# Seven products of quarters for the wide layers of five blocks instead of three, and larger steps of side work

## The chip, the cores and the metric

The kernel runs on one core of a Trainium2 chip. The metric is the device time of one execution in microseconds. A profile of one execution goes with it; its span runs from the first to the last instruction.

## What is computed

The program is a "macaron" layer on x of 4 x 1024 x 256 floats: half a feed-forward step, a mixing step over time, and half a feed-forward step again, each with a layer norm in front and a residual behind.

```python
def ffn(x):                      # w1_w, w2_w, h1_w, h2_w, w3_w hold -1, 0, 1
    h = silu(tlin(x, w1)) * tlin(x, w2)      # 256 -> 1024
    h = gelu(tlin(h, h1))                    # 1024 -> 1024, "wide"
    h = gelu(tlin(h, h2))                    # 1024 -> 1024, "wide"
    return tlin(h, w3)                       # 1024 -> 256
def attn(x):                     # a convolution over time by FFT, then one more product
    K = s4d_kernel(...)
    y = irfft(rfft(x) * rfft(K))[:L]
    return gelu(y) @ W.T + b
x = x + 0.5 * ffn(norm(x))
x = x + attn(norm(x))
x = x + 0.5 * ffn(norm(x))
```

Each `tlin` also scales its outputs by a vector.

## The kernel before, in words

**Blocks.** The 4096 tokens are cut into 8 blocks of 512 (TB). They pass the first feed-forward step as f0 to f7 and the second as g0 to g7; the mixing step of batch b, called m0 to m3, lies between: it needs f(2b) and f(2b+1), and g(2b), g(2b+1) need it. The last loop of `macaron_layers` runs `ffn` for f0 to g7 in turn. `x1` and `x2` in DRAM carry what one step hands to the next.

**A block.** Activations are split into a high and a low part, so that each product is done twice and summed in PSUM (`linear`, L366). The pair of first layers writes banks `pa` and `pb`; layers 2 and 3 (weights `h1_sb`, `h2_sb`) write `p2_...` and `p3_...`, eight pieces m of 128 output rows each, and each piece is 16 matmuls of 512 columns. A piece goes through Gelu on ACT (L418), a cast on ACT to the high part (L420) and a subtraction on DVE to the low part (`low_part`, L309). A following layer needs all eight. The last layer (L630) writes `po`. `ffn` calls `ahead()` and `tick()` after each piece of a wide layer. `ahead` takes a step of `prepare` for the next block: its load, its norm, its transposition through DRAM (`moved`, stored and loaded on POOL's queue).

**Blocks by sums.** In the last N_BY_SUMS blocks the wide layers are done by `winograd`: weights and activations are halved in both directions, and seven products of quarters (names `a`, `d`, `e` in `p2a_g`, `p3d_g` and so on, L484) replace eight. A product is 32 matmuls of 256 columns. Seven sums of weight quarters per wide layer are made once by `weight_sums` (16 steps in all; each second step stores seven pieces of `q` in DRAM, on POOL's queue). A block by sums loads 14 parts of 1 MB through SP's queue into four slots (`load_slot`, L581). Slots and activation tiles of these blocks take the place of `h1_sb` and `h2_sb`, so all sums must be made, and all mixing steps be done (an `assert` says so), when the first block by sums begins. Sums not made by then are made at that point, all at once.

**Side work.** `all_aside` is a generator that makes the convolution's spectrum (`kernel_steps`, `kernel_spectrum`) and then m0 to m3 in small steps. Work on DVE is counted in columns plus OP_WORK = 130 for each operation. Each `tick` allows STEP_WORK more of it (STEP_WORK_2 once f7 is done) and takes steps until that is used up, or until a step yields PAUSE, which means that it waits for something. At a PAUSE, also when side work has run out or waits for its block, one step of the "fillers" is taken if enough allowance is left. Fillers are the 16 steps of `weight_sums` and then 46 of `weight_checks`: 44 pieces of the weights are loaded once more from their inputs (`given`, SP's queue, 256 KB each), and DVE compares each with what the kernel uses (L156); for the pieces of h1 and h2 it is compared with its own sign, which ACT makes (L714). A value `bad` counts misses, and a plain version of the whole kernel runs behind an `If` where there are any.

**Order.** Within an engine the instructions stand in an order that the tile framework's scheduler fixes when the program is built; each engine works through its own in order. So where a matmul of the next layer needs a low part that comes late, the program may have put other matmuls in front of it.

**Lines that matter here:** L38 (steps), L44 (N_BY_SUMS), L309 and L366 (low part, products), L418 and L420 (Gelu, cast), L484 (products of quarters), L581 (weight parts), L630 (last layer), L703 and L714 (checks: load, sign), and `tick`.

Of the kernel before, what the change touches and what calls it, by code (L numbers as in the profile page):

```python
# [24 lines left out]
TB = 512  # L25
# [9 lines left out]

STEP_WORK, STEP_WORK_2, OP_WORK, MIN_WORK = 2500, 3000, 130, 300  # L38
PAUSE = "pause"
N_CHECKS = 44  # L40

N_BY_SUMS = 3  # L44
QT = TB // 2
QK = KH // 2
QW = HID // 2
# [62 lines left out]
def macaron_layers(  # L110
# [37 lines left out]
    work_done = 0  # L148
# [213 lines left out]
    def linear(ps, w, m, acts):  # L362
        n = len(acts)
        for k in range(n):
            for part in range(parts):
# [6 lines left out]
                )  # L372

    def ffn(xt, src, dst, blk, name, tick, ahead, final, by_sums):


# [21 lines left out]
        for layer, w in ((2, h1_sb), (3, h2_sb)):  # L398
            if by_sums:
                at = 0  # L400

                def step():
                    nonlocal at
                    at += 1
                    if at * KH // 14 > (at - 1) * KH // 14:
                        ahead()
                        if layer == 2 or at < 14:
                            tick()

                raw = winograd(raw, layer, name, step)  # L410
                continue
            hb = []
            for m in range(KH):
                ps = bank(f"p{layer}_{name}_{m}")
                linear(ps, w, m, ha)
                t = ring(f"h{layer}_{name}_{m}", parts, TB, dtype=wide)
                g = half(f"g{layer}_{name}_{m}") if split else t[:, 0, :]
                nc.scalar.activation(g, ps, AF.Gelu, scale=sc_sb[:, layer, m : m + 1])  # L418
                if split:
                    nc.scalar.copy(t[:, 0, :], g)  # L420
                    low_part(t, g)
                hb.append(t)
                ahead()
                if layer == 2 or m < KH - 1:
                    tick()
            ha = hb
# [91 lines left out]
    def winograd(raw, layer, name, step):  # L518
# [51 lines left out]
        (quarters[layer][i], f"w_{n}_{layer}_{i}")  # L570
        for n in range(N_BY_SUMS)
        for layer in range(2)
# [620 lines left out]
    done = []  # L1193
# [50 lines left out]
    fillers = chain(sums_of_weights, checks) if split else iter(())  # L1244
    late = late_pool = None
    ticks = 0
    allowed = 0

    def tick():


        nonlocal ticks, allowed, work_done
        ticks += 1
        allowed = min(allowed, work_done) + (
            STEP_WORK_2 if ("f", n_blocks - 1) in done else STEP_WORK
        )
        while work_done < allowed:
            at = work_done
            if next(aside, PAUSE) is PAUSE:
                if len(done) > 8 and allowed - work_done > OP_WORK + TB:  # L1260
                    next(fillers, None)
                break
            if work_done == at:
                work_done += MIN_WORK
# [8 lines left out]
    allowed = work_done  # L1273
    for n, (turn, blk) in enumerate(blocks):
# [8 lines left out]

        by_sums = split and n >= len(blocks) - N_BY_SUMS
        if by_sums and not slots:
# [93 lines left out]
```

## Time and profile before

| | |
|---|---|
| median of the runs | 1400.81 us (1399.09 to 1400.86, 3 runs) |
| the profiled execution | 1398.44 us, of which the span is 1396.7 |
| granted TensorE clock | 0.999 |
| matmuls of 512 columns in layers 2 and 3 | 1024 + 1024 in f0 to f7, 640 + 640 in g0 to g4 |
| Gelu behind them (L418), one | 689 ns on ACT |
| cast (L420) / low part (L309), one | 618 ns on ACT / 690 ns on DVE |
| a load of ACT's function table | 1283 ns |
| Sign of a check (L714) / compare (L156), one | 627 ns on ACT / 686 ns on DVE |
| weight part `w<-q`: count, size, issue to landing | 42, 1024 KB, 6.1 us |
| check load `given<-in_h_dram`: count, size, issue to landing | 32, 256 KB, 5.0 us |
| moved by DMA | 160.11 MB, mean 115 GB/s |

Times of single operations are means of groups of equal instructions. "Busy" of TensorE (PE) counts matmuls, which overlap, so that a matmul's own duration (391 ns for 512 columns) is longer than the step from one to the next; PEld are the loads of weights into the array, which run beside matmuls. An idle time of an engine is put down to the event that ended it.

The blocks begin at about these times of the span (first matmul of `pa`): f0 10, f1 90, f2 176, f3 259, f4 354, f5 441, f6 521, f7 622, g0 702, g1 796, g2 883, g3 977, g4 1063, g5 1157, g6 1238, g7 1314 us.

### The profile page before, as it was taken

To read this page: it belongs to the slowest core of one execution; us is meant where nothing else is said; L and a number is where in the kernel's file an instruction comes from. 1 tells how busy PE (TensorE), PEld (TensorE's weight loads), DVE (VectorE), ACT (ScalarE), POOL (GpSimd) and SP (SyncE) were. 2 spreads that over 40 slices of the span, in tenths; PEclk is the share of its full clock that TensorE was granted. 3 is DMA by queue.
4 is the path that set the end of the run, shared out by engine and by line. 5 is a ranking of instruction groups with operands and counts; after the bars stand their busy time and mean duration, and the time that the engine had idled before them with its cause. 6 is when DMAs were issued, how large, how long until landed. Compare 5 with 4: busy or idle time off the path is not lost.

```text
span 1396.7 us, 19695 instructions
## 1 busy us (share of the span) xinstructions
PE 1384.2 (99%) x7132; PEld 1182.6 (85%) x7132; DVE 932.8 (67%) x1766; ACT 766.8 (55%) x1227; POOL 297.0 (21%) x454
## 2 busy tenths in 40 slices
PE   9999999999999999999999999999999999999998
PEld 7888888888888888888888888888888888989998
DVE  6896667755637776377774569844597536877765
ACT  5986579644546445354353544534544445766664
POOL 4441022211312121521125301221112032121200
PEclk9999999999999999999999999999999999999999
DMA  9430101113131331532314414233132356959663
GB/s 355 127 131 21 41 16 46 31 30 96 50 108 36 106 90 54 203 92 83 76 46 162 134 37 128 61 91 106 53 95 50 100 143 237 332 169 320 193 221 114
DMA packets 121677, 160.11 MB, mean 115 GB/s; under 512 B 73873, under 2 KB 84113, under 8 KB 116193
## 3 DMA queue, kind: packets, MB, share of 16 engines
q1 hardware_dynamic: 99296, 99.41, 23.5%
q0 software_dynamic: 22000, 59.07, 13.7%
q8 instruction: 58, 0.95, 0.3%
q14 instruction: 51, 0.41, 0.1%
q10 hardware_dynamic: 272, 0.26, 0.1%
HBM read 120.95 MB, written 37.75 MB: 114 GB/s over the span
## 4 chain that ended last, share of the span: by engine, by line
PE 93%; DVE 3%; DMA 2%; ACT 1%; issue 0%; POOL 0%; SPq 0%; DVEq 0%; POOLq 0%; ACTq 0%
PE p_f L366 31%; PE p_g L366 19%; PE pa_f L366 4%; PE pa_g L366 4%; PE pb_f L366 4%; PE pb_g L366 4%; PE po_f L630 4%; PE po_g L630 4%; PE p2a_g L484 3%; PE p3a_g L484 3%; PE pi L1144 2%; PE pw L1169 2%; PE pf_m L966 2%; PE p2d_g L484 1%; PE p3d_g L484 1%; PE pk L893 1%
## 5 line engine op out<-in xcount | busy, mean ns | idle before, releaser
L366 PE MATMUL p_f<-h_f,h_sb 128*128 128x512 f32 x1024 | 237.1, 391 | 0.0
L366 PE MATMUL p_f<-ha_f,h_sb 128*128 128x512 f32 x1024 | 235.3, 390 | 0.0
L366 PEld LDWEIGHTS p_f<-h_f,h_sb 128*128 128x128 f32 x1024 | 191.8, 188 | 40.0 <-DVE h_f L309 0.3
L366 PEld LDWEIGHTS p_f<-ha_f,h_sb 128*128 128x128 f32 x1024 | 191.9, 188 | 39.8
L418 ACT ACTIVATE g_f<-p_f,sc_sb 128x512 f32<-128x512 f32 x128 | 87.7, 689 | 190.5 <-PE p_f L366 186.0
L309 DVE TENSOR_TENSOR h_f<-g_f,h_f 128x512 fp32r<-128x512 f32 x128 | 87.7, 689 | 143.3 <-ACT h_f L420 142.9
L418 ACT ACTIVATE g_g<-p_g,sc_sb 128x512 f32<-128x512 f32 x80 | 55.2, 690 | 174.6 <-PE p_g L366 165.0
L366 PE MATMUL p_g<-ha_g,h_sb 128*128 128x512 f32 x640 | 148.1, 391 | 0.0
L366 PE MATMUL p_g<-h_g,h_sb 128*128 128x512 f32 x640 | 147.9, 391 | 0.1
L366 PEld LDWEIGHTS p_g<-h_g,h_sb 128*128 128x128 f32 x640 | 120.0, 188 | 25.4 <-ACT h_g L420 0.5
L366 PEld LDWEIGHTS p_g<-ha_g,h_sb 128*128 128x128 f32 x640 | 120.0, 188 | 24.7
L309 DVE TENSOR_TENSOR h_g<-g_g,h_g 128x512 fp32r<-128x512 f32 x80 | 55.2, 690 | 111.8 <-ACT h_g L420 111.3
L339 POOL DMA_DIRECT2D moved<-sq_g x64 | 34.9, 552 | 314.9 <-DVE sq_g L156 313.8
L420 ACT CAST h_f<-g_f 128x512 fp32r<-128x512 f32 x128 | 78.3, 618 | 2.9
L418 ACT ACT_TABLE_LOAD x46 | 59.0, 1283 | 20.9 <-PE p_f L366 12.4
L366 PE MATMUL pa_f<-xt_f,w_sb 128*128 128x512 f32 x256 | 69.0, 390 | 0.7 <-DVE xt_f L321 0.7
L366 PE MATMUL pb_f<-xt_f,w_sb 128*128 128x512 f32 x256 | 68.8, 389 | 0.0
L366 PE MATMUL pa_g<-xt_g,w_sb 128*128 128x512 f32 x256 | 68.5, 389 | 0.0
L366 PE MATMUL pb_g<-xt_g,w_sb 128*128 128x512 f32 x256 | 68.4, 389 | 0.0
L392 DVE SCALAR_TENSOR_TENSOR g_g<-pb_g,sc_sb,g_g 128x512 f32<-128x512 f32 x64 | 47.7, 748 | 29.9 <-PE pb_g L366 19.2
L339 POOL DMA_DIRECT2D moved<-sq_f x56 | 30.8, 556 | 159.1 <-DVE sq_f L156 159.1
L392 DVE SCALAR_TENSOR_TENSOR g_f<-pb_f,sc_sb,g_f 128x512 f32<-128x512 f32 x64 | 47.3, 746 | 23.0 <-PE pb_f L366 15.9
(310 smaller groups left out, 2493.9 us busy)
## 6 DMA issues: line engine op xcount, KB each, us to landing
w<-q SPq DMA_DIRECT2D x42, 1024.0 KB, 6.1
q<-s POOLq DMA_DIRECT2D x40, 256.0 KB, 3.4
h_sb<-in_h_dram POOLq DMA_DIRECT2D x8, 1024.0 KB, 14.6
given<-in_h_dram SPq DMA_DIRECT2D x32, 256.0 KB, 5.0
kr<-k_hat SPq DMA_DIRECT2D x20, 256.0 KB, 2.7
ki<-k_hat SPq DMA_DIRECT2D x20, 256.0 KB, 2.9
xr_f<-in_x_dram SPq DMA_DIRECT2D x64, 64.0 KB, 2.5
q<-h_sb POOLq DMA_DIRECT2D x16, 256.0 KB, 5.8
```

Of the source, the lines that this page charges most:

```text
L309: return nc.vector.tensor_tensor(t[:, 1, :], src, t[:, 0, :].bitcast(F32), ALU.subtract)
L339: stores.dma_start(moved[k].rearrange("(c r) a q -> a r c q", r=SQ)[a], sq[a * SQ : (a + 1) * SQ].rearrange("r c j s -> r c (j s)"),)
L366: nc.tensor.matmul(ps, w[:, k, m * P : (m + 1) * P], acts[k][:, part, :], start=(k == 0 and part == 0), stop=(k == n - 1 and part == parts ...
L392: nc.vector.scalar_tensor_tensor(g if split else t[:, 0, :], pb, sc_sb[:, 1, m : m + 1], g, ALU.mult, ALU.mult)
L418: nc.scalar.activation(g, ps, AF.Gelu, scale=sc_sb[:, layer, m : m + 1])
L420: nc.scalar.copy(t[:, 0, :], g)
L484: nc.tensor.matmul(ps[:, e * QT : (e + 1) * QT], weights[:, c, m * P : (m + 1) * P], ops[c // 2][:, part, c % 2 * QT : (c % 2 + 1) * QT], ...
L630: nc.tensor.matmul(ps[:, n * n_t : (n + 1) * n_t], w3_sb[:, k, o * P : (o + 1) * P], act(k, part, n * n_t, (n + 1) * n_t), start=(k == ord ...
L893: nc.tensor.matmul(pk[0:NA, at + i, :, :].rearrange("p h b -> p (h b)"), a[:, i].rearrange("p a b -> p (a b)"), qd[d1 // per_tile][:, at + ...
L966: nc.tensor.matmul(ps[e][:, part, :], m[:, e, part, :], rows_of(q + JQ * e), start=True, stop=True)
L1144: nc.tensor.matmul(banks[dc][e][:, q * P : (q + 1) * P], vs[q + JQ * e][:, part, dc * P : (dc + 1) * P], m[:, e, part, :], start=(part == ...
L1169: nc.tensor.matmul(ps[:, e * D : (e + 1) * D], yts[dc][j // JQ][:, (j % JQ + e) * P : (j % JQ + e + 1) * P], wt_sb[:, dc, :], start=(dc == 0),
```

## The change

N_BY_SUMS goes from 3 to 5: g3 and g4 are done by sums too, so the mixing steps and the sums of weights have to be made two blocks earlier. The allowance of a tick grows from 2500 to 3200 columns, and from 3000 to 3400 once f7 is done. At a PAUSE up to two filler steps are taken instead of one, as long as the allowance lasts.

```diff
-STEP_WORK, STEP_WORK_2, OP_WORK, MIN_WORK = 2500, 3000, 130, 300
+STEP_WORK, STEP_WORK_2, OP_WORK, MIN_WORK = 3200, 3400, 130, 300
...
-N_BY_SUMS = 3
+N_BY_SUMS = 5
...
             if next(aside, PAUSE) is PAUSE:
-                if len(done) > 8 and allowed - work_done > OP_WORK + TB:
-                    next(fillers, None)
+                for _ in range(2):
+                    if len(done) > 8 and allowed - work_done > OP_WORK + TB:
+                        next(fillers, None)
                 break
```

What a filler step does is unchanged: the same 16 steps of sums and 46 of checks are made once.

## The prediction

> **What bounds the kernel now.** I read four views, in this order. First the page's totals and its 40 slices: which engine is full, and where.
>
> ```profile
> PE 1384.2 (99%) x7132; PEld 1182.6 (85%) x7132; DVE 932.8 (67%) x1766; ACT 766.8 (55%) x1227; POOL 297.0 (21%) x454
> ...
> PE   9999999999999999999999999999999999999998
> PEld 7888888888888888888888888888888888989998
> DVE  6896667755637776377774569844597536877765
> ACT  5986579644546445354353544534544445766664
> ...
> PEclk9999999999999999999999999999999999999999
> ```
>
> TensorE is full from end to end at full clock, so the time is the sum of its matmuls plus what it waits. The other rows are below 7 on average, but reach 8 and 9 in slices 2 to 4, 7 and 25: there they are almost the bound. Only in the last six slices does PEld reach 9: those are the blocks by sums.
>
> Second, the chain of waits, in order of time: what a pair of wide layers costs in both forms, and the last layer behind it.
>
> ```profile
> 455.57 58.03 PE p_f L366 x256
> 513.60 7.25 PE po_f L630 x32
> ...
> 1306.31 7.68 PE po_g L630 x64
> 1328.52 3.83 PE p2a_g L484 x32
> 1332.35 3.84 PE p2d_g L484 x32
> ```
>
> Third, the busy time by stretch for the blocks g5, g6, g7, the three already done by sums, each from its first matmul to the next block's.
>
> ```profile
> 1157.40:1237.50 80.10, 77.94 (x577) 73.87 (x576) 59.62 (x110) 56.16 (x107) 12.85 (x20) 1.00 0.81 283
> 1237.50:1313.80 76.30, 76.30 (x580) 73.62 (x580) 57.33 (x108) 50.77 (x96) 13.44 (x21) 1.00 0.73 241
> 1313.80:1390.00 76.20, 76.15 (x578) 73.43 (x576) 49.05 (x77) 48.23 (x91) 8.89 (x11) 1.00 0.45 157
> ```
>
> The columns are length, then busy time of PE, PEld, DVE, ACT, POOL, then clock, DMA share, GB/s. The same matmuls take 80.1 us in g5 and 76.2 in g6 and g7. Fourth, the waits of g5 alone (1157 to 1238) say why:
>
> ```profile
> DVE given L156 <- ACT sign L714: 7.0, 5, 2.1
> ...
> ACT sign L714 <- DMA given<-in_h_dram: 5.2, 5, 1.4
> ```
>
> Fifteen weight checks run in g5. Their 256 KB loads stand in SP's queue just behind 1 MB loads of weight parts and land after 6.8 us (median), against 3.3 in g3 and g4. ACT, which works in order, sits on a check's Sign while casts for the next product stand behind it. DVE waits next, and then TensorE, about 4 us in all. Over the blocks before g5, TensorE's only visible waits are 0.7 us at the first matmuls and 0.3 in f2.
>
> **The change, part by part.**
>
> *Two more blocks by sums (g3, g4).* Each drops 256 + 32 matmuls of 512 columns: 58.03 + 7.25 = 65.28 us by the chain, 227 ns each. Each gains 14 products of 32 matmuls of 256 columns at 3.84 us (120 ns each), and 64 in the last layer at 7.68: 53.76 + 7.68 = 61.44. That is 3.84 us a block, **7.7 us** for two, and all of it on the engine that sets the end. The Trainium skill, "TensorE: Matmul & The Clock Gate", in the part "Wait — 56ns, not 53.3ns?", prices a warm matmul at its columns by 2.4 GHz plus about 2.5 ns: 215.7 ns for 512 columns, 109.2 for 256. By that, 1024 x 109.2 - 576 x 215.7 = -12.4 us. The trace has 120, not 109, and PEld is busy 27.0 of 27.0 us in the products (1355 to 1382): weight loads, twice as many per column, fill the stage. I take the trace.
>
> The added DVE and ACT work lies beside these matmuls: g7 has the same work at 49 us DVE and 48 ACT of 76, g6 with seven checks 57 and 51, and neither waits. The 28 more loads of 1 MB on SP follow the pattern of g6 and g7 too, each hidden by four slots.
>
> *Larger steps (2500 to 3200, 3000 to 3400), two fillers at a pause.* These have to bring all side work in front of g3, since the weights h1, h2 are given up there. Going through the program block by block, the last mix ends in g2, all 16 steps of weight sums are done by f7, and of 62 filler steps 61 are done by g2 (25 of them in g2) and one in g3. So nothing is left to drain at the entrance to g3. Three costs follow.
>
> (a) *g5's wait goes.* No check's load stands among weight loads any more: 80.1 - 76.2 = **3.9 us** gained. Ends: 0 (if it belongs to the first block by sums rather than to the checks) and 4.1. The waits name the checks, so 3.9.
>
> (b) *g2 takes 25 filler steps, mostly pairs.* Per layer piece of 3.63 us a pair adds two Signs (0.63 each) to ACT's 0.69 + 0.62, so 2.6 us, and two compares (0.69) to DVE's 0.69, so 2.1: both fit. Each pair's 512 KB in 3.6 us is 144 GB/s, with no weight loads about. What can go wrong is the second load of a pair, needed right after the first: ACT and the casts and Gelus behind Sign would wait, then TensorE. Below: 0, as g4 with its ten steps shows (no Sign waits for a load there). Above: g5's rate, 3.9 x 25 / 15 = 6.5 us. Nearest is g4, since the 19-buffer ring lets loads run some ticks ahead; I take 0.3. SP's queue in g2 also holds the mix's x1 rows and the next blocks' x behind those loads; none is due before g5.
>
> (c) *f0 to g1 get denser.* A tick goes with 3.63 us of wide-layer matmuls (58.03 / 16). 3200 units are about five 512-column DVE operations: 5 x 0.61 (their spacing in the chain) = 3.05, plus low part 0.61 and about 0.5 for the next block: 4.2 us, where 2500 gave 3.5. So ticks in a row without a pause fall behind; pauses and side matmuls give it back. By counted instructions times row durations, DVE has 695 us up to g2's third layer against 930 of PE (before: 729 against 1090 up to g4): full only in places. In f0, between the last low part of the first layer and that of the third, DVE gets 12 more operations of 512 columns and four of 256: about 8 us on top of 49.2 busy in 58.2 (24.2 to 82.4). Part of the 9 us of idle there are waits for ACT that stay. Before, the last low part ended at 86.0, 3.8 us behind its matmuls; 2 to 5 more make 6 to 9. The program's PE order puts 26 matmuls (5.9 us) in between, where it was 16: a wait of 0 to 3, I take 1.8. In f1's third layer ACT gets 11 table loads at 1.30, 16 Gelus and casts at 0.69 and 0.62, nine Exp/Sin at 0.62, eight tap copies at 0.2: 32.0 us against 30.1 of PE; order there leaves 6.4 us: I take 0.7. Here the skill speaks against the change: "ScalarE: Activation LUTs", "What ACT_TABLE_LOAD costs", gives 1283 ns plus a drain of some 1380, 2.66 us a switch; then ACT would need 46.9 us and TensorE would lose over 10. The trace shows the next ACTIVATE 1.30 us after a load's start (241.33 to 242.63), and f2, with 21 loads in two layers, lost 0.3 us in all. So 1.30. The other full layers (f4, f5, f6, f7, g0, g1; DVE 28 to 31 us against 29 to 33) get 0.7 together: g1 before ran DVE at 61.0 of 72.7 us with TensorE losing under 0.1. Sum 3.2; ends 0 and 9 (about 3 us for f0, 2 for f1, 4 elsewhere).
>
> (d) *Entrance to g3.* The first parts are loaded when g2's third layer ends, as at g4 to g5 before (loads at 1150.21, first product at 1171.89 without a wait). One now stands in front of eight residual loads on SP, which held it up to 9 us; 21.7 us of matmuls cover that. Nothing.
>
> **Sum**, on the profiled execution (1398.44 us; span 1396.7): -7.7 - 3.9 + 0.3 + 3.2 = -8.1, so 1390.3. The median shown is 1400.81, 0.17% above that execution; the same ratio gives **1392.7**.
>
> **Rivals** (times on the median's scale).
>
> *The dense front hardly costs* (chance 0.2): the order hides f0 and f1 as it hid f2. For it, f2's 0.3. Against it, f0's DVE has no room. -11.6 + 0.3: 1389.5.
>
> *g5's extra time belongs to the entrance* (0.07) and shows up in g3: -8.1 + 3.9 = -4.2: 1396.6.
>
> *Pairs of checks hold ACT in g2* at g5's rate (0.13): +6.2 on my sum, -1.9: 1398.9, no change.
>
> *Slower: DVE and ACT become the bound in the front* (0.1). Place: layers two and three of f0 to g1, eight of which hold 27.7 us or more of DVE or ACT work. Each would have to give TensorE a wait at its end, as the layer's last low part comes after its side work. Beyond 14 us in all it outweighs 11.6 plus the threshold; at 2.5 us each, 20: -11.6 + 20 = +8.4: 1409.2. For it, slices 2 to 4 at 8 and 9; against it, g1 at 843 to 876 with DVE at 32.6 of 33 and almost no wait.
>
> That the change doesn't do what it says is excluded by the program: 576 matmuls of 512 columns are gone, 1024 of 256 are there.
>
> My forecast keeps 0.5. Within 0.2% (2.8 us) is what a measurement can't tell from no change, so faster means under 1398.0. Faster: 0.5 x 0.97 + 0.2 + 0.06 + 0.05 = 0.8; same 0.09 (mainly the pairs); slower 0.11. The range reaches from the front costing nothing, less scatter, to the pairs' case: 1387 to 1399.5.
>
> **What would show it.** Blocks g3 to g7 at 76.2 us each, g5 among them; PE busy down by about 8 + 2 us; no Sign waiting for a load after g3's start; first waits of TensorE at the ends of f0's and f1's third layers, on low parts. It is wrong if f0 to g1 hold more than 9 us of TensorE waits, if g2 is long through Sign, or if g3 takes 80.

## The result and the profile after

| | before | after |
|---|---|---|
| median of the runs, side by side | 1400.58 us (1399.09 to 1400.86, 6 runs) | 1388.32 us (1386.70 to 1388.67, 6 runs) |
| profiled execution, its span | 1398.44, 1396.7 us | 1388.35, 1386.6 us |
| loads of weight parts, 1 MB each | 42 | 70 |

The ratio of after to before is 0.9915, with a 95% interval of 0.9905 to 0.9925: 10.5 to 13.3 us faster. The forecast was 1392.7.

Totals and slices of the kernel after:

```profile
PE 1375.9 (99%) x7580; PEld 1197.6 (86%) x7580; DVE 983.1 (71%) x1846; ACT 792.6 (57%) x1306; POOL 296.7 (21%) x454
...
PE   8999999999999999999999999999999999999998
PEld 7888888888888888888888888888899999999998
DVE  6997778465696558975688656984576775666765
...
PEclk9999999999999999999999999999999999999999
```

TensorE is still full at full clock, so most of the shorter time is fewer matmul microseconds: 1375.9 against 1384.2 busy, 8.3 of the 10.1 us between the spans; the other 1.8 are less waiting. PEld had four 9s near the end; now there are ten in a row: these are the five blocks by sums. VectorE reads 9 in slices 2 and 3 already: the front has less room than it had.

Busy time by stretch for g3, g4 and g5, each from its first matmul to the next block's (length, then PE, PEld, DVE, ACT, POOL, clock, DMA share, GB/s):

```profile
1000.40:1076.60 76.20, 76.20 (x580) 73.53 (x579) 51.27 (x81) 48.40 (x92) 13.26 (x20) 1.00 0.76 262
1076.60:1152.60 76.00, 76.00 (x578) 73.48 (x577) 56.07 (x94) 50.04 (x95) 13.82 (x21) 1.00 0.70 230
1152.60:1228.50 75.90, 75.90 (x578) 73.39 (x577) 50.54 (x79) 48.95 (x92) 12.66 (x20) 1.00 0.66 221
```

All three take 76 us and PE is busy in all of it. Before, g3 and g4 took 79.8 and 80.1 once the mixing step's matmuls between them are taken off, and g5 80.2. (Blocks with no side matmul give the measure: f5 before takes 79.79 us, so the side matmuls in a block of 86.7 us like f4 cost 6.9, and those in one of 93.9 us like g2 14.1.) These three blocks give about 3.7 + 4.2 + 4.2 = 12.1 us. The checks that stood in g5 now stand in g2, between 931 and 991 us; g2 takes 93.88 us as before, and no Sign in it waits for a load: ACT's one wait at a Sign there is 0.8 us for a buffer.

The waits of TensorE over the whole span (who waited, for whom, total, times, longest) have two lines that matter:

```profile
PE pa_f L366 <- DVE xt_f L321: 0.7, 1, 0.7
...
PE p_f L366 <- DVE ha_f L309: 0.3, 1, 0.3
```

The first was there before. The second is new, at the first wide layer of f1 (at 110 us), where it ends a chain of VectorE work that goes back to 82 us.

Since side matmuls move between blocks, the front is compared as a whole. f0 to g2 before, with the 21.0 us of side matmuls that it left to g3 and g4, come to 988.3 us; after, with 0.2 left, 990.7. So the front costs 2.4 us in this profile. Of that some 1.4 us is no cost of the change: the profile after shows a clock of 0.60 from 9.9 to 14.0 us, where the profile before shows 1.00, and the first eight matmuls of `pa` and `pb` take about 0.2 us longer each; the run with the steps alone, below, has the same start without that. With g6, which is 0.3 shorter, the account closes: -12.1 + 2.4 - 0.3 = -10.0, against -10.1 between the spans. (f0 begins 0.4 us later after, and g7 is 0.4 shorter to the last instruction; the two cancel.)

### The profile page after: what moved, and what is told of

Same layout as the page of the kernel before. It is cut to its first block, busy times and chain, and to the rows that moved or that the text cites. A ratio compares the mean times of both kernels' runs of the same rounds, so it can differ in the third digit from the quotient of the medians.

```text
span 1386.6 us, 20804 instructions
## 1 busy us (share of the span) xinstructions
PE 1375.9 (99%) x7580; PEld 1197.6 (86%) x7580; DVE 983.1 (71%) x1846; ACT 792.6 (57%) x1306; POOL 296.7 (21%) x454
## 4 chain that ended last, share of the span: by engine, by line
PE 94%; DVE 3%; ACT 1%; issue 1%; DMA 0%; DVEq 0%; ACTq 0%
PE p_f L366 31%; PE p_g L366 13%; PE p3a_g L484 6%; PE p2a_g L484 6%; PE pa_g L366 4%; PE pb_g L366 4%; PE po_g L630 4%; PE pa_f L366 4%; PE pb_f L366 4%; PE po_f L630 3%; PE p2d_g L484 3%; PE p3d_g L484 3%; PE pi L1144 2%; PE pw L1169 2%; PE pf_m L966 2%; PE p3e_g L484 1%
## 5 line engine op out<-in xcount | busy, mean ns | idle before, releaser
L366 PE MATMUL p_g<-ha_g,h_sb 128*128 128x512 f32 x384 | 89.2, 391 | 0.0
L366 PE MATMUL p_g<-h_g,h_sb 128*128 128x512 f32 x384 | 88.6, 391 | 0.0
L366 PEld LDWEIGHTS p_g<-h_g,h_sb 128*128 128x128 f32 x384 | 71.9, 188 | 15.3 <-DVE h_g L309 0.4
L366 PEld LDWEIGHTS p_g<-ha_g,h_sb 128*128 128x128 f32 x384 | 72.0, 188 | 14.9
L418 ACT ACTIVATE g_g<-p_g,sc_sb 128x512 f32<-128x512 f32 x48 | 33.1, 689 | 85.0 <-PE p_g L366 78.2
L391 ACT ACTIVATE g_g<-pa_g,sc_sb 128x512 f32<-128x512 f32 x64 | 43.7, 688 | 41.4 <-PE pa_g L366 41.3
L418 ACT ACT_TABLE_LOAD x42 | 53.9, 1283 | 16.6 <-PE p_f L366 10.5
```

What stands on the lines that cost most here:

```text
L366: nc.tensor.matmul(ps, w[:, k, m * P : (m + 1) * P], acts[k][:, part, :], start=(k == 0 and part == 0), stop=(k == n - 1 and part == parts ...
L391: nc.scalar.activation(g, pa, AF.Silu, scale=sc_sb[:, 0, m : m + 1])
```

## The experiments

Each is a small edit of one of the two kernels. My theory is the prediction's sum: the sums of quarters give 3.84 us a block, g5's extra time goes because the checks leave it, and the front costs a few us. What is told apart first is where g5's 4.2 us came from.

**The steps alone.** The kernel after, with three blocks by sums as before:

```diff
-N_BY_SUMS = 5
+N_BY_SUMS = 3
```

> The changed kernel with three blocks by sums, as before: only the steps and the pairs of fillers are new. My theory: the checks are done before g5, so g5 takes 76.2 us in place of 80.1, the dense front costs about 1 us, and the time falls by about 3 us, to some 1397.5. Rival (the extra time of g5 belongs to the entrance into the blocks by sums): g5 stays at 80, and the time is 1400.6 or a little above. Rival (the larger steps bring the main gain by themselves): 1392 or less.

Measured: 1394.35 us, ratio 0.9958 (0.9941 to 0.9974). The median falls by 5.7 us, twice what I expected; the span of the profiled execution falls by 3.4. Its g5, in the same view:

```profile
1158.50:1234.50 76.00, 76.00 (x578) 73.49 (x577) 52.27 (x80) 48.26 (x92) 13.25 (x20) 1.00 0.76 261
```

The first block by sums takes 76 us without checks in it, so the 4.2 us do not belong to the entrance: that rival falls, and so does the one that had the larger steps bring the main gain. From this kernel to the one after, only g3 and g4 change: 80.15 to 76.24 and 79.79 to 75.97, which is 7.7 us for two blocks by sums. Its front, the same program as after's and without the slow first matmuls, is 1.1 us over the front of before. By an estimate f0 gives +0.5, f1 some +1.4 and the rest -0.8 in sum. (It takes 2.2 us for a `pk` product of 32 matmuls, from f1 before: 86.4 us with three of them, where a block without takes 79.8.)

**One filler at a pause.** The kernel after, with the pairs undone, so that 27 comparisons that stood in g2 and before, and with them the sum of their misses, come to stand in g3 and g4:

```diff
-                for _ in range(2):
+                for _ in range(1):
```

> The changed kernel with one filler at a pause instead of up to two: 15 filler steps then fall into g3 and 13 into g4, among the loads of weight parts. My theory: Sign waits for loads there as it did in g5, some 0.26 us lost for each check, so g3 and g4 take about 80 and 79 us and the time is about 7 us above the changed kernel's 1388.3: 1395. Rival (pairs hold ACT in g2 and cost there what they save): about the changed kernel's time, 1388.

Measured: 1398.3 us, ratio 0.9986 (0.9974 to 0.9998). The stretches of g3 and g4, then their waits for check loads and TensorE's longest:

```profile
998.70:1079.80 81.10, 78.36 (x578) 74.03 (x577) 60.31 (x111) 56.96 (x108) 13.63 (x21) 1.00 0.85 296
1079.80:1162.30 82.50, 78.69 (x580) 75.24 (x579) 60.53 (x119) 54.04 (x103) 13.19 (x21) 0.98 0.73 246
```

```profile
ACT sign L714 <- DMA given<-in_h_dram: 10.4, 7, 4.3
...
PE p3d_g L484 <- ACT t1s_g L465: 3.0, 1, 3.0
```

Five blocks by sums, and nearly all the gain is gone: g3 is 4.8 and g4 6.6 us longer than after, 11.4 for 28 steps, 0.41 each. I had taken g5's rate, 0.26, so the direction was right and the size too small. PE is idle for 6.5 of these us, and one wait of 3.0 on an activation half (`t1s`) is behind ACT. Behind that wait the granted clock is 0.76 and 0.81 in the next two stretches of 4 us, some 1.7 us lost. So without the edit from one filler to two, which looks like the smallest part of the change, 10.0 of the 12.3 us are lost. That is its worth where five blocks are done by sums: with three, pairs and larger steps together gave 5.7, and no run parts the one from the other.

**No checks.** The kernel before, without the 44 comparisons:

```diff
-        following = load(0)
+        nc.vector.memset(miss, 0.0)
...
-        for n, (src, held) in enumerate(todo):
+        for n, (src, held) in enumerate(todo[:0]):
```

> The kernel before without the 44 comparisons of weights (their loads, Signs and compares are left out, and the count of misses is set to zero). My theory: g5 takes 76.2 us and nothing else changes by more than 0.3 us, so the time falls by 4 us to about 1396.6. Rival (g5's extra time belongs to the entrance): no change. A fall of clearly more than 4 us would mean that checks cost elsewhere too, in g0 to g4.

Measured: 1394.86 us, ratio 0.9964 (0.9949 to 0.9978). g5 takes 76.7 us in place of 80.2, and the matmuls of no other block move by more than 0.3 (what follows the last matmul of g7 takes 1.1 longer). So 3.5 of the 4.2 us are the checks' own. The other 0.7 is a stall of TensorE at the last layer, with a visible wait of 0.5; the low part that it needs stands on DVE behind a cast for the next block, which waits for its load:

```profile
PE po_g L630 <- DVE hl_g L309: 0.5, 1, 0.5
```

```profile
1230.53 0.43 DVE L356 CAST xt_g<-xf_g 128x512 fp32r<-128x512 f32 x1 [3.54 <-DMA xf_g<-moved]
```

In the kernel before no such cast stands there, so the checks may account for all of its 4.2 us.

**Check loads on the other queue.** The kernel before, with `given` loaded through GpSimd's queue, so that no weight part stands in front of it:

```diff
-            nc.sync.dma_start(given, todo[n][0])
+            nc.gpsimd.dma_start(given, todo[n][0])
```

> The kernel before with the loads of the checks issued on GpSimd's queue instead of SP's. If the place behind weight loads in SP's queue makes the check loads late, they land in about 3.3 us again, no Sign waits, g5 takes 76.2 us and the time falls by 4 us to 1396.6. If it is the DMA engines themselves, which are shared with the 1 MB loads, they land as late as before (6.8 us) and g5 stays at 80; GpSimd's queue, where the stores stand, could make it worse, up to 1405.

Measured: 1400.72 us, ratio 1.0008 (0.9999 to 1.0017); g5 is 83.2 us, 3.0 longer. Two waits of g5:

```profile
POOL given L703 <- DVE given L156: 25.2, 6, 7.3
...
PE po_g L630 <- ACT hl_g L465: 4.6, 1, 4.6
```

The loads of g5 now land after 4.3 us (median) in place of 6.8, and the waits of Sign that the profile puts down to a load fall from 5.2 us to 1.6. So much of the lateness came with the place in SP's queue. But the queue of GpSimd now stands at buffers that earlier checks give back, and at other transfers, and its last check loads land after 9.1 and 7.6 us. The second of these lands at 1227.0 in the trace. A Sign follows 0.1 us later, behind 2.9 us of idle ACT for which the profile names no event, and casts for the last layer stand behind it:

```profile
1227.11 0.63 ACT L714 ACTIVATE sign<-given 128x512 f32<-128x512 f32 x1 [2.91 <-issue]
```

Together with the 1.6 us at the Sign before, that is the size of the one wait of 4.6 us at the last layer. The clock behind it is low:

```profile
1229.80:1233.80 4.00, 3.99 (x17) 3.76 (x18) 3.45 (x6) 3.28 (x7) 0.00 (x0) 0.50 0.89 256
1233.80:1238.00 4.20, 4.20 (x34) 4.20 (x34) 2.21 (x5) 0.00 (x0) 0.00 (x0) 0.89 0.43 71
```

At these clocks 2.0 + 0.5 us are lost. The whole of g5 but for that one place takes 83.2 - 4.6 - 2.5 = 76.1 us by this estimate, like a block without checks. So of the expectation's two cases the one with the queue holds for most of g5, but two late loads were enough to undo the gain.

**Check loads earlier.** The kernel before, with four loads ahead instead of one:

```diff
-        following = load(0)
+        coming = [load(n) for n in range(4)]
...
-            given = following
-            if n + 1 < len(todo):
-                following = load(n + 1)
+            given = coming.pop(0)
+            if n + 4 < len(todo):
+                coming.append(load(n + 4))
```

> The kernel before, with each check's load issued four steps ahead of its use instead of one. If Sign waits only because the load comes late behind 1 MB loads, none waits now, g5 falls from 80.2 to about 76.5 us, and the time by about 3.7 to some 1396.5. If it is the checks' own work on ACT and DVE (15 Signs and compares, 20 us) that delays the casts in g5, g5 stays near 80 and the time at 1400.

Measured: 1399.29 us, ratio 0.9993 (0.9984 to 1.0001). In g5 no Sign waits for a load any more, and yet g5 takes 81.8 us. Its longest wait of TensorE, the compare behind which that low part stands, and the stretches behind the wait:

```profile
PE po_g L630 <- DVE hl_g L309: 2.8, 1, 2.8
```

```profile
1229.00 0.69 DVE L156 SCALAR_TENSOR_TENSOR given<-given,w_sb 128x512 f32<-128x512 f32 x1 [3.04 <-DMA given<-in_w_dram]
```

```profile
1230.30:1234.00 3.70, 3.64 (x18) 3.65 (x19) 3.70 (x9) 0.50 (x1) 0.00 (x0) 0.54 1.04 374
1234.00:1238.00 4.00, 4.00 (x36) 4.00 (x35) 2.50 (x6) 0.33 (x1) 0.00 (x0) 1.00 0.68 108
```

The compare waits 3.0 us for its load of `w3`: with 17 checks in g5 in place of 15, this one comes before the last layer is done. That too is a late load, on DVE instead of ACT. At a clock of 0.54 in 3.7 us another 1.7 are lost. Without these two, g5 would take 81.8 - 2.8 - 1.7 = 77.3 us by this estimate, where a block without checks takes 76.0. What remains, about 1.3 us, goes with two waits of 0.3 at `p2d_g` and `p3d_g`, which stay from the kernel before although nothing waits for a load there. The run with the other queue left nothing for them. So of g5's 4.2 us some 3 to 4 belong to late loads, and at most 1.3 to the checks' own work on ACT and DVE. This split is an estimate; no run kept every load early.

**Larger steps, to find the edge of the front.** The kernel after with 5000, then 8000, columns a tick in the dense blocks. The slower rival put the edge at 14 us of waits at the ends of the layers.

```diff
-STEP_WORK, STEP_WORK_2, OP_WORK, MIN_WORK = 3200, 3400, 130, 300
+STEP_WORK, STEP_WORK_2, OP_WORK, MIN_WORK = 5000, 3400, 130, 300
```

> The changed kernel with 5000 columns a tick up to f7 in place of 3200. A tick then holds about eight DVE operations of 512 columns, 6 us of DVE against 3.63 us of matmuls. My theory (the order hides a lag up to the last layer's length, about 6 us): f0 to f3 now wait at their ends, 2 to 3 us each, so about 8 us more than the changed kernel: 1396. Rival (the dense front costs next to nothing at any step, since pauses give it back): 1388 to 1389. Rival (DVE as the bound): over 1400.

> The changed kernel with 8000 columns a tick up to f7. My theory: twelve DVE operations a tick, side work of f0 to f2 packed as densely as it goes; 20 us or more of waits in f0 to f6, 1408 or more. Rival (pauses give it back): below 1395.

Measured: 1464.38 us, ratio 1.0463 (1.0445 to 1.0482), and 1524.82, ratio 1.0895 (1.0877 to 1.0913). The rival's mechanism exists. At 5000, TensorE waits 17.2 us in nine waits at `po_f` for low parts, as the rival said; but one single wait of 13.3 us is at `pk`, a matmul of the spectrum, and I had named no such thing. The next run looks nearer to 3200.

> The changed kernel with 4200 columns a tick up to f7. At 3200 f0 to f2 lost some 1.5 us, at 5000 the kernel lost 76 us. If that loss begins where a tick's DVE work passes the 3.63 us of its matmuls by more than pauses give back, 4200 (6.5 operations, 5.1 us) already loses much: 1400 to 1430. If it begins with something that only 5000 does (the spectrum's matmuls placed in front of their operands), 4200 stays below 1395.

Measured with 4200: 1430.56 us, ratio 1.0212 (1.0195 to 1.0229). A third more allowance costs 42 us, where going from 2500 to 3200 had cost about 1. Behind its first matmuls TensorE has five gaps over 1 us: 12.1 and 9.7 at `pk`, and 3.6, 1.1 and 3.9 at `po_f`. Two lines of its timeline, TensorE's and VectorE's (start, length, engine, line, operation; in brackets the idle time before it and its releaser):

```profile
87.45 1.89 PE L893 MATMUL pk<-qd,p 128*64 128x32 f32 x16 [12.12 <-DVE p L156]
```

```profile
86.62 0.69 DVE L156 TENSOR_TENSOR p<-p,po 128x512 f32<-128x512 f32 x1
```

The stretch of the gap and the one behind it:

```profile
76.00:86.00 10.00, 0.00 (x0) 0.00 (x0) 9.95 (x22) 9.86 (x14) 1.28 (x3) 0.64 0.42 170
86.00:94.00 8.00, 6.55 (x41) 5.47 (x41) 7.93 (x16) 4.66 (x6) 0.00 (x0) 0.59 0.01 2
```

The product `pk` takes 1.89 us for its 16 matmuls and nobody needs it soon. But it stands in TensorE's order in front of the wide layer's matmuls, and its operand `p` is made by VectorE, which is busy for 9.95 of 10 us and gets to it at 86.6. Ready matmuls stand behind it for 12 us. The clock is 0.59 over the 8 us in which the gap ends. Between two gaps, in 110 to 140 us, it is 1.00 again.

How near was the kernel after? Of the eight `pk` products of 32 matmuls, the one with the least time in hand for its first half, and the `p` that this half needs; it is the same product in before and after:

```profile
284.12 2.05 PE L893 MATMUL pk<-qd,p 128*64 128x32 f32 x32
```

```profile
277.01 0.69 DVE L156 TENSOR_TENSOR p<-p,po 128x512 f32<-128x512 f32 x1
```

```profile
221.73 2.05 PE L893 MATMUL pk<-qd,p 128*64 128x32 f32 x32
```

```profile
219.86 0.68 DVE L156 TENSOR_TENSOR p<-p,po 128x512 f32<-128x512 f32 x1
```

Before, the operand was there 284.12 - 277.70 = 6.4 us ahead; after, 221.73 - 220.54 = 1.2 us. No wait of the kernel after shows that: only the spacing of the two lines does. How far this order is from one that loses is not shown. (For any half the least is 2.8 us before and 0.8 after.) In the run with 3600 columns below, the program places the products elsewhere: the least is 5.2 us for a first half and 2.1 for any, and no `pk` waits. So the allowance alone doesn't set the time in hand; where the scheduler puts the product does too.

**The product one piece later.** To see whether it is the place of `pk` that costs, 4200 again with the products let in when six results are ready, not four; the first then stands one piece (16 matmuls) later in TensorE's order.

```diff
-                if len(ready) == 4:
+                if len(ready) == 6:
```

> The kernel after with steps of 4200 columns in the dense blocks, as in the run before, but the spectrum's products (pk) are let into a step only once six results of their inputs are ready instead of four, so that the first of them stands two steps later in TensorE's order. If the loss at 4200 comes from a side product that stands in TensorE's queue ahead of its operand (12.3 and 9.9 us of gaps, and the half clock that follows them), most of it goes: 1400 to 1410 us, and no gap over 5 us at a pk product. If VectorE is behind as such, whichever product stands there waits instead: 1425 to 1431 us, with gaps of the same sum at the po, p_f or pk products.

Measured: 1419.06 us, ratio 1.0143 (1.0124 to 1.0162), between the two expectations. The product starts when it did in the run with 4200 before, behind a shorter gap:

```profile
87.13 1.89 PE L893 MATMUL pk<-qd,p 128*64 128x32 f32 x16 [8.48 <-DVE p L156]
```

The gap shrinks from 12.12 to 8.48 us, by 3.64, and a piece is 3.63: the operand comes when it came (87.3 and 87.1), and the matmuls that now stand in front of the product fill the gap. In place of the second gap of 9.7 us stand two of 0.9 and 1.4, less by 7.4, about two pieces. Both theories were too simple. The place of the product decides how much of VectorE's delay TensorE feels, so "another product waits instead" is wrong (the gaps fall from 31 to 20 us in sum); but at 4200 VectorE's delay is larger than one piece can cover, so the loss does not go either.

**Six blocks by sums.** Can the gain be carried on? First with 4600 in the late blocks and three fillers, then with 3600 and 4600 and two, then with 5000, the checks' loads four ahead and their last sum held back by 24 steps.

```diff
-STEP_WORK, STEP_WORK_2, OP_WORK, MIN_WORK = 3200, 3400, 130, 300
+STEP_WORK, STEP_WORK_2, OP_WORK, MIN_WORK = 3200, 4600, 130, 300
...
-N_BY_SUMS = 5
+N_BY_SUMS = 6
...
-                for _ in range(2):
+                for _ in range(3):
```

> Six blocks by sums, steps of 3200 and 4600, up to three fillers at a pause; all side work and all checks are then done by the end of g1. My theory: g2 saves another 3.84 us of matmuls; g0 and g1 hold what g0 to g2 held, DVE about 10 us more each, which fits into g0's 94 us and lags in g1, cost 0 to 3 us: 1385 to 1388. Rival (g0 and g1 become bound by DVE): 1390 or more.

> Six blocks by sums as in the run before, but with steps of 3600 and 4600 and two fillers at a pause: side work lies earlier, so g1 is nearly free of it and the front is denser. My theory: -3.84 us against the changed kernel, 1 to 4 us more of waits in f0 to f2: 1385.5 to 1388.5. If it beats the run before, g1 was what cost there; if it loses, the front is.

> Six blocks by sums with steps of 3200 and 5000, two fillers at a pause, checks loaded four steps ahead, and the matmul that adds up the misses held back by 24 filler steps. The run with six blocks lost 9.8 us in g1: 4.9 on that matmul, 2.0 on a matmul of the mix, the rest on checks. My theory: those go, but for 2 to 3 us; g2 saves 3.84: 1386 to 1387.5. Rival (g1 is bound by DVE with or without the checks' waits): 1390 or more.

Measured: 1395.08 (ratio 0.9969, 0.9959 to 0.9979), 1405.97 (1.0043, 1.0026 to 1.0060) and 1394.70 (0.9967, 0.9955 to 0.9978): all slower than the kernel after. In the first, g1 is 9.8 us longer: TensorE waits 4.8 us at the matmul that adds up the checks' misses, for VectorE, and 1.8 at one of the mixing step. In the second the loss is not in the front, where its expectation looked for it, but in g0, which is 16 us longer than its matmuls account for: TensorE waits 6.9 us at its last layer and 7.3 at the first matmul of g1. In the third the sum of misses is out of the way, and g1 is still 10.9 longer; its stretches, and TensorE's longest wait in them:

```profile
802.00:832.00 30.00, 30.00 (x135) 24.93 (x134) 23.32 (x48) 15.44 (x24) 4.56 (x6) 1.00 0.30 70
832.00:862.00 30.00, 30.00 (x134) 24.86 (x133) 28.86 (x56) 16.23 (x24) 3.23 (x5) 1.00 0.32 98
862.00:892.00 30.00, 23.69 (x114) 18.80 (x113) 28.19 (x52) 8.38 (x14) 0.00 (x0) 0.83 0.25 77
```

```profile
PE p_g L366 <- DVE h_g L309: 5.4, 2, 3.3
```

VectorE is at 28.9 and 28.2 of 30 us, while ACT and the DMA have room. TensorE is still full in the first 60 us; in the last 30 it is idle for 6.3, mostly for two low parts, and the clock is 0.83. So it is VectorE that bounds the end of g1. In these three forms, having the side work done one block earlier costs more than the 3.84 us that a block gives back.

## Why the prediction was right

The direction and both large gains held, with their sizes. The cost of the front and the step from the profile to the median did not; all errors were on the same side and added up to 4.4 us, so the measured 1388.3 lies near the fast end of the stated range.

*Two more blocks by sums, -7.7.* Right. The steps-alone run and the kernel after differ by 3.9 and 3.8 us in g3 and g4, one block each. The Trainium skill, "TensorE: Matmul & The Clock Gate", in the part "Wait — 56ns, not 53.3ns?", would have made it -12.4 by the prediction's estimate. In the kernel after a product of 32 matmuls takes 3.84 us again, 120 ns each, with PEld at 73.5 of 76 us: taking the row instead of the rule was the right choice.

*(a) g5's wait goes, -3.9.* The size was right (-4.2) and so was the cause in its coarse form: the checks made it. Late loads make most of it, as the prediction said: 3 to 4 us by the estimates above. That they are the whole of it, and through ACT's Sign alone, is not shown: up to 1.3 us can be the checks' own work, and a late load at a compare on DVE did the same harm.

*(b) Pairs in g2, +0.3.* Nothing was lost: g2 is 93.88 us in both kernels. The check loads of that stretch land after 4.1 us (median). The rival that had pairs hold ACT in g2 fell.

*(c) The denser front, +3.2: the mis-sized step.* It costs 1.1 us in the steps-alone run, and 2.4 with 1.4 of slow first matmuls in the profile after. f0, for which I took 1.8, gave 0.5. VectorE fell behind there as forecast: the last low part of its third layer ends at 90.5, 6.6 us behind the layer's matmuls, inside my 6 to 9. But the order of matmuls hid it, and the place where I put the wait shows a gap of 0.2. f1 gave some 1.4 where I took 0.7, and its longest wait is at the first wide layer, not behind the third. The other full layers, 0.7 together in the forecast, cost nothing: the blocks from f2 on gave back some 0.8. My reading of the slices was loose too: slice 4 of VectorE and ScalarE is at 6, and those at 8 and 9 stand in 2, 3, 7, 25, 26, 30 and 35. The table loads of f1 did not come through to TensorE: no wait of TensorE for ACT is left in the front of the trace after, as the row of 1.30 us a load had it. The rival "the dense front hardly costs", 1389.5, ends nearest to the measured time.

*(d) The entrance.* g3 takes 76.0 us net: nothing, as said.

*From the profile to the median.* By the profiled executions the change gives 10.1 us where the sum had 8.1. The 2.0 between them are (b) and (c) with 1.1 (2.4 for 3.5, slow first matmuls included), (a) and g6 with 0.3 each, the blocks by sums with 0.2, and 0.1 of rounding. The median had another 2.2 us: I carried over that the median of before lies 0.17% above its profiled execution, but the median of after equals its own (1388.32 and 1388.35).

*The slower rival* had VectorE as the next bound, and that is so: at 4200 the loss outweighs the gain. But its place was only half right. Low parts at the layers' ends waited (8.5 us in the 4200 run); the larger waits (22 us) were at side products, which the program puts in front of matmuls that are ready.

## What to carry to other kernels

Where one engine is full and works in order, an added or hastened side product costs by its place: compare when its operand is made with when its turn comes, and the difference is the margin. The least margin went from 6 to 1 us here without any wait to show it. Steps larger by a third then cost 42 us. But ask for the margin again after each change, since the order changes with it: in the run with 3600 columns it was 5 again.

Moving small loads and comparisons away from the stretch in which large transfers and a full weight path run can be worth as much as a better algorithm: without one line, two fillers at a pause, 10 of the 12 us were lost.

Before carrying a ratio from one profiled execution to a median, allow for the executions' own scatter: 2 us here, as large as several steps of the sum.

## What the runs showed of the hardware

TensorE's granted clock falls behind a long gap and takes some microseconds to come back. In the 4200 run it is 0.59 over the 8 us in which the 12-us gap ends, in the 5000 run 0.58, and there eight matmuls of 512 columns behind the 13.3-us gap take 3.71 us, 464 ns each against 227. So a gap costs more than its length. The Trainium skill, in the page "TensorE: Matmul & The Clock Gate", section "What's actually happening", has the clock fall to a half after an idle window of about 3.4 us; the gaps here of 8.5 us and more agree. Shorter ones did it too: 2.8 us with the loads four ahead (0.54 in the 3.7 us behind it), 3.0 in g4 with one filler (0.76 in the 4 us behind it), and, with the products one piece later, two of 0.9 and 1.4 us with a small product between them (0.50 from 185 to 189 us). A wait of 0.8 in g5 of the kernel before left the clock at 1.00. How short a single gap may be is not settled, but 3.4 us is not the least.

Moving loads to another queue was no gain by itself: through GpSimd's queue the check loads landed sooner in the middle (4.3 us against 6.8), but the last ones took 9.1 and 7.6 us, and g5 was 3.0 us longer.
